# Mixture of experts on TensorE: fixed weight-stationary pairs of tiles ahead of the register-addressed blocks

## The chip, the cores and the metric

The kernel runs on one core of a Trainium2 chip. The metric is the device time of one execution, in microseconds (us). The engines are called PE (TensorE, matmuls; its weight loads are listed apart as PEld), DVE (VectorE), ACT (ScalarE), POOL (GpSimd) and SP (SyncE, which here only issues DMAs).

## What is computed

One transformer layer on 2048 tokens of width 256, all in float32: causal attention with 16 heads, a residual and a layer norm, then a mixture of experts, a residual and a second layer norm. The change touches the mixture of experts only:

```python
scores = softmax(t @ gate_w.T)            # 2048 tokens, 16 experts
weights, indices = top_k(scores, 2)
for e in range(16):                       # INTER = 176, DIM = 256
    w_e = sum(where(indices == e, weights, 0))
    y += (silu(t @ w1[e].T) * (t @ w3[e].T)) @ w2[e].T * w_e
z = (silu(t @ sw1.T) * (t @ sw3.T)) @ sw2.T    # shared expert, width 352
out = layernorm(x + y + z)
```

Every token goes to two experts, so there are 4096 rows of expert work, 256 per expert on average; how many each gets depends on the data.

## The kernel before

**Up to the experts.** Attention fills the time up to about 605 us. Its work is an order written out by hand (`steps`, `at`, lines 590 to 738); the tokens are handled in four chunks of 512, and the last chunk to be finished is chunk 2 (`LAST`). After a chunk's layer norm, `choose` and `settle` compute each token's two experts, its two gates, and its row in `xg`, a DRAM buffer with room for 2048 rows per expert. `scatter` (L275) sends the rows of 128 tokens to `xg` with one indirect DMA from POOL. A row holds 256 values, the number of the row in `yg` to which the result goes, and the token's first expert. `xg` is filled with blank rows early on (L386). The weights `w1` and `w3` of all experts come in four loads into `w13` (L370), 2 x 176 columns per expert; `w2` comes in two loads into `w2r` (L748), as two halves of 88 rows.

**Around the experts.** The shared expert's pieces (`shared_hidden`, L780, and `shared_out`, L796) serve as work for PE while something else is waited for: chunks 3 and 0 and a first piece of chunk 1 come before the experts, the rest of chunk 1 and chunk 2 after them. `shared_out` writes x + shared expert into a tile `z`. `table` (L816) works out from the counts which expert each block of 128 rows belongs to (`own`), the first row of the block in `xg` (`row`) and the number of blocks (`total`). `keys` (L852) gives each block's expert number on all partitions.

**The blocks.** An expert with n rows takes ceil(n / 128) blocks, one after the other over all experts. `in_turn` (L994) runs blocks 0 to 41 (`OFTEN` = 42), and then, under `tc.If` (L1014), blocks 42 to 46 when `total` is over 42. One block is:

- `load_block` (L867): SP loads the block's first row into a register (L868) and issues the load of 128 rows of `xg` into `xb` (L874), some eight blocks ahead (`DEPTH` = 6, eight buffers).
- `turn` (L879): two transposes on PE into `px`, one copy on DVE into `xbT`.
- `hidden` (L886): PE loads the expert's number into a register (L887); two matmuls, with `xbT` as the stationary operand and the expert's 352 columns of `w13`, addressed by that register, as the moving one, into `ph` (128 tokens x 352). ACT takes silu of the first 176 columns (`ru`, L901), DVE multiplies with the other 176 (`rh`, L903).
- `turn_hidden` (L905): two transposes of `rh` into `pT`, one ACT copy into `hT`.
- `output` (L914): two matmuls of `hT` with the expert's `w2r`, by register, into `py`; an ACT copy into `yb`; DVE works out the rows to write (`to`, L925); POOL scatters the rows into `yg` (L931). `to` and `yb` have three buffers each, so the fourth waits until a scatter has landed.

A float32 matmul of this kind is two PE instructions, a transpose is one. The program order of PE is kept (`pe`, L139, through which every matmul passes, hence line 140 in the profile); the other engines' order is chosen by the framework's scheduler. DMA loads that are marked with `keep_in_program_order` keep their order too.

**After the experts.** `fetch` (L937) loads `yg` back once all scatters have landed; `combine` (L947) adds two rows times their gates to `z` on DVE, and the layer norm and the store follow.

Of the kernel before, what the change touches and what calls it, by code (L numbers as in the profile page):

```python
# [10 lines left out]
F32 = mybir.dt.float32  # L11
I32 = mybir.dt.int32
# [15 lines left out]
NEXP, INTER, SHARED = 16, 176, 352  # L28
NF = NEXP * INTER
FTOT = NF + SHARED  # L30
HK = INTER // 2
SCH = [(0, P), (P, P), (2 * P, SHARED - 2 * P)]
NSC = len(SCH)
TT = S // P
ROW = E + 2

NBLK = (2 * S - NEXP) // P + NEXP
WARM = 3
LAST = 2
OFTEN = 42  # L40
DEPTH = 6
SCALE = 0.25
EPS = 1e-5
NEG = -1.0e30
# [3 lines left out]
def block_kernel(  # L48
# [96 lines left out]
    def transpose(*args):  # L145
        pe(nc.tensor.transpose, *args)
# [139 lines left out]
    with ExitStack() as att:  # L286
# [80 lines left out]
        for g in range(1, G):  # L367
            load_weights(g, nc.sync)
        nc.sync.dma_start(out=gw, in_=gate.rearrange("(k p) n -> p k n", p=P))
        for j, w in ((0, w1), (1, w3)):  # L370
            for k in range(2):
                nc.sync.dma_start(
                    out=w13[:, k, :, j * INTER : (j + 1) * INTER],
                    in_=w[k * P : (k + 1) * P, :NF].rearrange("p (n f) -> p n f", f=INTER),
                )

        def load_shared():
# [364 lines left out]
    fp2 = ctx.enter_context(tc.tile_pool(name="fp2", bufs=2))  # L742
    fp3 = ctx.enter_context(tc.tile_pool(name="fp3", bufs=3))
    fp4 = ctx.enter_context(tc.tile_pool(name="fp4", bufs=4))
    fp8 = ctx.enter_context(tc.tile_pool(name="fp8", bufs=8))
    ps_a = ctx.enter_context(tc.tile_pool(name="ps_a", bufs=2, space=PSUM))

    w2r = fp1.tile([HK, 2, NEXP, E], F32, tag="w2r", name="w2r")  # L748
    for j in range(2):
        nc.sync.dma_start(  # L750
            out=w2r[:, j],
            in_=w2[:NF, :].rearrange("(n j q) e -> j q n e", j=2, q=HK)[j],
        )

    blocks = fp1.tile([P, 1], F32, tag="blocks", name="blocks")
# [13 lines left out]
        out=upto, in_=upto, pattern=[[1, NEXP], [-1, NEXP]], base=0, channel_multiplier=0,  # L769
        compare_op=ALU.is_ge, fill=0.0,  # L770
    )

    z = fp1.tile([P, TT, E], F32, tag="z", name="z")

    def spare(name):
        return ps_a.tile([P, CH], F32, tag="t", name=name)

# [18 lines left out]
    def shared_out(c):  # L796
        for half in range(2):
            pz = ps_a.tile([P, 2, E], F32, tag="y", name=f"pz{c}_{half}")
            for t in range(2):
                o = (2 * half + t) * P  # L800
                for i, (_, m) in enumerate(SCH):
                    matmul(
                        pz[:, t, :], lhsT=hs[c, i][:m, o : o + P], rhs=sw2[:m, i, :],
                        start=(i == 0), stop=(i == NSC - 1),
                    )
            nc.vector.tensor_tensor(
                z[:, 4 * c + 2 * half : 4 * c + 2 * half + 2, :], pz,
                xr[c][:, 2 * half : 2 * half + 2, :E], ALU.add,
            )

    def shared(c):
        for i in range(NSC):
# [2 lines left out]

    def table():  # L816

        count = fp1.tile([P, NEXP], F32, tag="count", name="count")
        nc.vector.tensor_tensor(count, fill, room, ALU.subtract)
        whole = fp1.tile([P, NEXP], I32, tag="whole", name="whole")  # L820
        nc.vector.tensor_scalar(whole, count, float(P - 1), None, ALU.add)
        nc.vector.tensor_scalar(whole, whole, 7, None, ALU.logical_shift_right)
        nb = fp1.tile([P, NEXP], F32, tag="nb", name="nb")
        nc.vector.tensor_copy(nb, whole)
        ends = fp1.tile([P, NEXP, NEXP], F32, tag="ends", name="ends")
        nc.vector.tensor_tensor(
            ends, upto, nb.unsqueeze(1).to_broadcast([P, NEXP, NEXP]), ALU.mult
        )
        end = fp1.tile([P, NEXP], F32, tag="end", name="end")
        nc.vector.tensor_reduce(end, ends, AX.X, ALU.add)  # L830

        past = fp1.tile([P, NEXP], F32, tag="past", name="past")
        nc.vector.tensor_scalar(past, end, blocks, None, ALU.is_le)
        owner = fp1.tile([P, 1], F32, tag="owner", name="owner")
        nc.vector.tensor_reduce(owner, past, AX.X, ALU.add)
        nc.vector.tensor_tensor(past, past, nb, ALU.mult)
        first = fp1.tile([P, 1], F32, tag="first", name="first")
        nc.vector.tensor_reduce(first, past, AX.X, ALU.add)
        nc.vector.tensor_tensor(first, blocks, first, ALU.subtract)
        nc.vector.tensor_scalar(  # L840
            first, first, float(S // P - 1), float(P), ALU.min, ALU.mult
        )
        nc.vector.scalar_tensor_tensor(first, owner, float(S), first, ALU.mult, ALU.add)
        row = fp1.tile([P, 1], I32, tag="row", name="row")
        nc.vector.tensor_scalar(row, first, float(NEXP * S), None, ALU.min)
        own = fp1.tile([P, 1], I32, tag="own", name="own")
        nc.vector.tensor_scalar(own, owner, float(NEXP - 1), None, ALU.min)
        total = fp1.tile([P, 1], I32, tag="total", name="total")
        nc.vector.tensor_copy(total, end[:, NEXP - 1 :])
        return own, row, end, total  # L850
# [12 lines left out]
        return key  # L863

    xb, xbT, us, hT, expert = {}, {}, {}, {}, {}

    def load_block(b, row):  # L867
        r = nc.values_load(  # L868
            row[b : b + 1, 0:1], engines=[mybir.EngineType.SP],
            min_val=0, max_val=NEXP * S,  # L870
            skip_runtime_bounds_check_because="an expert below their number, a block of its room",
        )
        xb[b] = fp8.tile([P, ROW], F32, tag="xb", name=f"xb{b}")
        load = nc.sync.dma_start(out=xb[b], in_=xg[bass.ds(r, P), :])  # L874
        tc.keep_in_program_order(load)
        if b == 0:
            wait_for(scattered, load)

    def turn(b):  # L879
        px = ps_a.tile([P, 2, P], F32, tag="t", name=f"px{b}")  # L880
        for k in range(2):
            transpose(px[:, k, :], xb[b][:, k * P : (k + 1) * P], ident)
        xbT[b] = fp3.tile([P, 2, P], F32, tag="xbT", name=f"xbT{b}")
        nc.vector.tensor_copy(xbT[b], px)

    def hidden(b, own):  # L886
# [5 lines left out]
        for k in range(2):  # L892
# [4 lines left out]
                ],  # L897
                start=(k == 0), stop=(k == 1),
            )
        u = fp2.tile([P, INTER], F32, tag="ru", name=f"ru{b}")  # L900
        nc.scalar.activation(u, ph[:, :INTER], AF.Silu)  # L901
        us[b] = fp2.tile([P, INTER], F32, tag="rh", name=f"rh{b}")
        nc.vector.tensor_tensor(us[b], u, ph[:, INTER:], ALU.mult)  # L903

    def turn_hidden(b):  # L905
        pT = ps_a.tile([P, 2, P], F32, tag="t", name=f"pT{b}")
        for k in range(2):
            transpose(pT[:HK, k, :], us[b][:, k * HK : (k + 1) * HK], ident)
        hT[b] = fp3.tile([HK, 2, P], F32, tag="hT", name=f"hT{b}")
        nc.scalar.copy(hT[b], pT[:HK])  # L910

    back = []

    def output(b, key):  # L914
        py = ps_a.tile([P, E], F32, tag="y", name=f"py{b}")
        for k in range(2):
            matmul(
                py, lhsT=hT[b][:, k, :],
                rhs=w2r[:, k].rearrange("p n e -> p (n e)")[:, bass.ds(expert[b] * E, E)],
                start=(k == 0), stop=(k == 1),  # L920
            )
        yb = fp3.tile([P, E], F32, tag="yb", name=f"yb{b}")
        nc.scalar.copy(yb, py)  # L923
        to = fp3.tile([P, 1], I32, tag="to", name=f"to{b}")
        nc.vector.scalar_tensor_tensor(  # L925
            to, xb[b][:, E + 1 : ROW], key[:, b : b + 1], xb[b][:, E : E + 1],
            ALU.not_equal, ALU.add,
        )
        disjoint(
            back, "back",  # L930
            nc.gpsimd.indirect_dma_start(  # L931
                out=yg[:, :], out_offset=bass.IndirectOffsetOnAxis(ap=to[:, 0:1], axis=0),
                in_=yb, in_offset=None, bounds_check=2 * S - 1, oob_is_err=False,
            ).ins,
        )

    def fetch(h):  # L937

# [8 lines left out]
    def combine(h, got):  # L947
        m2 = fp2.tile([P, 2, 2], F32, tag="m2", name=f"m2_{h}")
        for t in range(2):
            i = 2 * h + t  # L950
            r = z[:, i, :]
            for j in range(2):
                nc.vector.scalar_tensor_tensor(  # L953
                    r, got[:, t, j, :], gates[:, j, i : i + 1], r, ALU.mult, ALU.add
# [10 lines left out]
        o = fp3.tile([P, 2, E], F32, tag="o", name=f"o{h}")  # L965
        for t in range(2):
            nc.scalar.activation(  # L967
                o[:, t, :], z[:, 2 * h + t, :], AF.Identity,
                bias=rs[:, 1, t : t + 1], scale=rs[:, 0, t : t + 1],
            )  # L970
        nc.sync.dma_start(
# [11 lines left out]
    settle(LAST, spare, both)  # L983
    for t in range(4):
        scatter(LAST, t)
    own, row, end, total = table()
    for b in range(DEPTH + 2):
        load_block(b, row)
    key = keys(end)
    shared_hidden(0, 1)  # L990
    shared_hidden(0, 2)
    shared_out(0)
    shared_hidden(1, 0)
    def in_turn(first, last):  # L994

        turn(first)
        turn(first + 1)
        for b in range(first, last):
            hidden(b, own)
            if b > first:  # L1000
                output(b - 1, key)
            turn_hidden(b)
            if b + 2 < last:
                turn(b + 2)
            if b + DEPTH + 2 < last:
                load_block(b + DEPTH + 2, row)
        output(last - 1, key)

    in_turn(0, OFTEN)
    blocks_in_all = nc.values_load(  # L1010
        total[0:1, 0:1], min_val=0, max_val=NBLK,
        skip_runtime_bounds_check_because="the sum of the experts' blocks, NBLK at most",
# [82 lines left out]
```

## Time and profile before

| what | value |
|---|---|
| median of 6 runs | 812.13 us (810.42 to 814.64) |
| the profiled execution: its time | 810.44 us |
| the profiled execution: its span | 808.7 us |
| mean granted clock of PE | 0.981 |
| first transpose of a block (`px`) | 640.5 us |
| first hidden matmul (`ph`) | 643.8 us |
| last output matmuls (`py`) begin | 765.3 us |
| shared expert goes on (`h`) | 767.7 us |
| scatters to `yg` | 42, the first at 650.6 us, the last at 767.1 us |
| instructions of PE | 5086 matmuls and transposes, 5086 weight loads |

The page gives busy time by engine, with the share of the span:

```profile
PE 779.4 (96%) x5086; PEld 363.2 (45%) x5086; DVE 546.5 (68%) x1489; ACT 445.2 (55%) x997; POOL 322.7 (40%) x557
```

It also cuts the span into 40 slices of 20.2 us. A digit is the busy share in tenths, and PEclk is the clock that was granted to PE. The experts are slices 32 to 38.

```profile
PE   6999999999999999999999999999999899999995
PEclk9999999999999999999999999999899999999999
DMA  5469999991000000001000000000225322222162
```

In groups and timelines a row names the line, engine and operation, the tile written and the tiles read, and the shape. A mean duration of a PE matmul is the time of its whole passage, which overlaps with the next one's.

### The profile page before, as it was taken

How to read it: one execution, taken by the hardware profiler on the slowest of the kernel's cores; microseconds unless marked ns; L12 is line 12 of the kernel's file. 1: busy time of each engine (PE TensorE's matmuls, PEld its weight loads, DVE VectorE, ACT ScalarE, POOL GpSimd, SP SyncE). 2: the span in 40 equal slices, each digit the busy share in tenths (PEclk: the TensorE clock that was granted, in tenths of full speed). 3: DMA queues.
4: the chain of work that ended last, by engine and by line, in shares of the span. 5: the costliest groups of instructions: out<-in, count | busy, mean ns of one | idle time of the engine just before them, and what ended most of it. 6: DMA issues, size and time to landing. Idle time of an engine off the chain costs nothing. (4 is left out here: it accounts for less than half of the span.)

```text
span 808.7 us, 14999 instructions
## 1 busy us (share of the span) xinstructions
PE 779.4 (96%) x5086; PEld 363.2 (45%) x5086; DVE 546.5 (68%) x1489; ACT 445.2 (55%) x997; POOL 322.7 (40%) x557
## 2 busy tenths in 40 slices
PE   6999999999999999999999999999999899999995
PEld 3443433444433344533344443453336466666543
DVE  2868888887677877688787778887575433333276
ACT  1143657387775877676786768856452033333345
POOL 2033524444454454545444545453551323333300
PEclk9999999999999999999999999999899999999999
DMA  5469999991000000001000000000225322222162
GB/s 146 130 176 328 298 292 296 305 303 46 2 1 1 2 1 2 2 19 36 1 2 1 1 2 1 1 2 27 73 62 141 111 74 86 81 85 69 36 223 90
DMA packets 67379, 71.90 MB, mean 89 GB/s; under 512 B 4736, under 2 KB 61539, under 8 KB 67302
## 3 DMA queue, kind: packets, MB, share of 16 engines
q1 hardware_dynamic: 62286, 61.77, 27.8%
q0 software_dynamic: 3552, 8.43, 3.0%
q10 hardware_dynamic: 1464, 0.72, 0.4%
q8 instruction: 42, 0.69, 0.4%
q14 instruction: 35, 0.29, 0.1%
HBM read 26.44 MB, written 45.78 MB: 89 GB/s over the span
## 5 line engine op out<-in xcount | busy, mean ns | idle before, releaser
L535 ACT ACTIVATE p<-s 128x512 f32<-128x512 f32 (+3 forms) x640 | 292.7, 540 | 132.6 <-PE m L140 77.4
L140 PE MATMUL m<-k,q 32*128 32x512 f32 (+3 forms) x1280 | 303.5, 565 | 0.8 <-DVE rot L423 0.5
L140 PE MATMUL s<-qa,k 32*128 32x512 f32 (+3 forms) x1280 | 282.4, 565 | 2.9 <-DVE avs L563 1.8
L490 DVE TENSOR_REDUCE pm<-m 128x1 f32<-128x512 f32 x384 | 237.5, 681 | 42.1 <-PE m L140 41.7
L567 POOL TENSOR_TENSOR avs<-avs,more 128x512 f32<-128x512 f32 (+3 forms) x125 | 136.8, 1094 | 166.6 <-ACT more L566 163.0
L140 PEld LDWEIGHTS s<-qa,k 32*128 32x128 f32 x1280 | 107.5, 186 | 121.0 <-ACT p L535 67.4
L140 PE MATMUL av<-p,v 128*32 128x512 f32 (+3 forms) x1280 | 156.9, 551 | 1.1 <-POOL p L539 0.7
L140 PEld LDWEIGHTS m<-k,q 32*128 32x128 f32 x1280 | 122.8, 183 | 44.0 <-issue 10.9
L485 DVE CUSTOM_DVE_ANT_0 m<-m,qmask 128x512 f32<-128x512 f32 (+3 forms) x256 | 118.2, 521 | 30.4 <-PE m L140 27.3
L566 ACT COPY more<-av 128x512 f32<-128x512 f32 (+3 forms) x125 | 65.6, 525 | 38.3 <-PE av L140 30.4
L539 POOL TENSOR_SCALAR_AFFINE_SELECT p<-p 128x128 f32<-128x128 f32 x256 | 70.3, 296 | 38.8 <-ACT p L535 36.9
L931 POOL DMA_INDIRECT yg<-yb,to x42 | 41.4, 985 | 90.0 <-ACT yb L923 49.6
L140 PEld LDWEIGHTS av<-p,v 128*32 128x32 f32 x1280 | 27.2, 109 | 105.5 <-ACT p L535 53.3
L140 PE MATMUL ph<-w,xbT 128*128 x168 | 62.0, 494 | 2.5 <-DMA xb<-xg 1.8
L903 DVE TENSOR_TENSOR rh<-ru,ph 128x176 f32<-128x176 f32 x42 | 14.2, 337 | 53.4 <-ACT ru L901 53.3
L140 PE MATMUL h<-xT,cs 128*128 128x512 f32 (+1 forms) x96 | 45.2, 616 | 3.5 <-ACT yb L923 1.3
L901 ACT ACTIVATE ru<-ph 128x176 f32<-128x176 f32 x42 | 13.3, 318 | 60.9 <-PE ph L140 60.9
L278 POOL DMA_INDIRECT xg<-xr,slot x32 | 31.0, 970 | 32.7 <-issue 21.4
L140 PE MATMUL py<-w2r,hT 88*128 x168 | 43.4, 380 | 0.7 <-ACT hT L910 0.7
L140 PEld LDWEIGHTS ph<-w,xbT 128*128 128x128 f32 x168 | 29.2, 193 | 21.3 <-issue 12.7
L428 POOL TENSOR_TENSOR k<-rot 128x512 f32<-128x512 f32 x16 | 20.3, 1266 | 43.6 <-DVE rot L426 43.6
L140 PEld LDWEIGHTS py<-w2r,hT 88*128 88x128 f32 x168 | 31.7, 189 | 12.0 <-ACT hT L910 1.2
(147 smaller groups left out, 632.1 us busy)
## 6 DMA issues: line engine op xcount, KB each, us to landing
xg<-hot SPq DMA_DIRECT2D x16, 2064.0 KB
w<-in_w_dram SPq DMA_DIRECT2D x4, 1408.0 KB
xb<-xg SPq DMA_DIRECT2D x42, 129.0 KB
got<-yg SPq DMA_DIRECT2D x8, 512.0 KB
w2r<-in_w_dram SPq DMA_DIRECT2D x2, 1408.0 KB
xr<-in_x_dram SPq DMA_DIRECT2D x4, 512.0 KB
out_dram<-o SPq DMA_DIRECT2D x8, 256.0 KB
cs<-in_rope_dram SPq DMA_DIRECT2D x16, 80.0 KB
```

What stands on the lines that cost most here:

```text
L140: tc.keep_in_program_order(op(*args, **kw))
L278: put = nc.gpsimd.indirect_dma_start(out=xg[:, :], out_offset=bass.IndirectOffsetOnAxis(ap=slot[:, j, i : i + 1], axis=0), in_=xr[c][:, t, ...
L428: nc.gpsimd.tensor_tensor(ks[g, c], tmp[:, 0, :], tmp[:, 1, :], ALU.add)
L485: nc.vector.tensor_tensor_reduce(out=ps[:, :n], in0=ps[:, :n], in1=qmask[:, CH - n :], scale=1.0, scalar=3.0 * NEG, op0=ALU.add, op1=ALU.m ...
L490: nc.vector.tensor_reduce(to, ps, AX.X, ALU.max)
L535: nc.scalar.activation(pr[:, n0:], ps[:, n0:], AF.Exp, scale=SCALE)
L539: nc.gpsimd.affine_select(out=diag, in_=diag, pattern=[[1, P]], base=0, channel_multiplier=-1, compare_op=ALU.is_ge, fill=0.0,)
L566: nc.scalar.copy(more[:, n0:], pv[:, n0:])
L567: nc.gpsimd.tensor_tensor(to, to, more[:, n0:], ALU.add)
L901: nc.scalar.activation(u, ph[:, :INTER], AF.Silu)
L903: nc.vector.tensor_tensor(us[b], u, ph[:, INTER:], ALU.mult)
L931: nc.gpsimd.indirect_dma_start(out=yg[:, :], out_offset=bass.IndirectOffsetOnAxis(ap=to[:, 0:1], axis=0), in_=yb, in_offset=None, bounds_c ...
```

## The change

The first 256 rows of every expert get a path of their own, at addresses that are known when the program is built. The pair of tiles is loaded, transposed (four transposes, one copy), and multiplied with the weights as the stationary operand and the 256 tokens as the moving one, so that the hidden values come out already turned: 112 + 64 rows of silu's argument and of the factor, in three pieces (`ab` twice, `c`). Silu and product give `hT` directly. The output matmuls take `hT` as the stationary operand, as before. The pair's results go back in two scatters. Sixteen experts run so, one after the other, with an expert's output after the next one's hidden part.

Only rows beyond 256 of an expert go through blocks with a register, by the old path. `OFTEN` is 10 now, `DEPTH` 2, and the part under `tc.If` holds blocks 10 to 27. The weight columns in `w13` are arranged as 112 + 64 + 64 + 112, so the silu of a block takes 240 columns, its product is cut in two, and the hidden transposes are of 112 and 64 columns with an ACT copy each. `w2r` is cut at 112 instead of 88, and `w13` comes in eight loads instead of four. `shared_out` adds into `xr` itself, `z` is gone. The table comes after the first four pair loads and the shared pieces in the program, and counts blocks beyond two per expert. The path is used with fewer than 256 rows too; blank rows are computed then, and not written.

```diff
-HK = INTER // 2
+H1, H2 = 112, INTER - 112
-NBLK = (2 * S - NEXP) // P + NEXP
+NBLK = 28
-OFTEN = 42
-DEPTH = 6
+OFTEN = 10
+DEPTH = 2
...
-            nc.vector.tensor_tensor(
-                z[:, 4 * c + 2 * half : 4 * c + 2 * half + 2, :], pz,
-                xr[c][:, 2 * half : 2 * half + 2, :E], ALU.add,
-            )
+            r = xr[c][:, 2 * half : 2 * half + 2, :E]
+            nc.vector.tensor_tensor(r, r, pz, ALU.add)
...
+    def load_two(e):
+        xb2[e] = fp4.tile([P, 2, ROW], F32, tag="xb2", name=f"xb2_{e}")
+        load = nc.sync.dma_start(
+            out=xb2[e], in_=xg[e * S : e * S + 2 * P, :].rearrange("(t p) r -> p t r", p=P)
+        )
+        tc.keep_in_program_order(load)
+        if e == 0:
+            wait_for(scattered, load)
+
+    def turn_two(e):
+        px = ps_a.tile([P, 2, 2, P], F32, tag="t", name=f"px2_{e}")
+        for k in range(2):
+            for t in range(2):
+                transpose(px[:, k, t, :], xb2[e][:, t, k * P : (k + 1) * P], ident)
+        xT2[e] = fp3.tile([P, 2, 2 * P], F32, tag="xT2", name=f"xT2_{e}")
+        nc.vector.tensor_copy(xT2[e], px.rearrange("p k t m -> p k (t m)"))
+
+    def hidden_two(e):
+        ab = ps_a.tile([P, 2, 2 * P], F32, tag="h", name=f"ab{e}")
+        c = ps_a.tile([P, 2 * P], F32, tag="c", name=f"c{e}")
+        for to, o, m in ((ab[:H1, 0], 0, H1), (c, H1, P), (ab[:H1, 1], INTER + H2, H1)):
+            for k in range(2):
+                matmul(
+                    to, lhsT=w13[:, k, e, o : o + m], rhs=xT2[e][:, k, :],
+                    start=(k == 0), stop=(k == 1),
+                )
+        u = fp2.tile([P, 2, 2 * P], F32, tag="u2", name=f"u2_{e}")
+        nc.scalar.activation(u[:H1, 0], ab[:H1, 0], AF.Silu)
+        nc.scalar.activation(u[:H2, 1], c[H2:], AF.Silu)
+        hT2[e] = fp2.tile([P, 2, 2 * P], F32, tag="hT2", name=f"hT2_{e}")
+        nc.vector.tensor_tensor(hT2[e][:H2, 1], u[:H2, 1], c[:H2], ALU.mult)
+        nc.vector.tensor_tensor(hT2[e][:H1, 0], u[:H1, 0], ab[:H1, 1], ALU.mult)
+
+    def output_two(e):
+        py = ps_a.tile([P, 2, E], F32, tag="y", name=f"py2_{e}")
+        for t in range(2):
+            for j, r in parts:
+                matmul(
+                    py[:, t], lhsT=hT2[e][r, j, t * P : (t + 1) * P], rhs=w2r[r, j, e],
+                    start=(j == 0), stop=(j == 1),
+                )
+        yb = fp3.tile([P, 2, E], F32, tag="yb2", name=f"yb2_{e}")
+        nc.scalar.copy(yb, py)
+        to = fp3.tile([P, 2, 1], I32, tag="to2", name=f"to2_{e}")
+        nc.vector.scalar_tensor_tensor(
+            to, xb2[e][:, :, E + 1 : ROW], float(NEXP - e), xb2[e][:, :, E : E + 1],
+            ALU.not_equal, ALU.add,
+        )
+        for t in range(2):
+            send_back(yb[:, t], to[:, t])
...
-        u = fp2.tile([P, INTER], F32, tag="ru", name=f"ru{b}")
-        nc.scalar.activation(u, ph[:, :INTER], AF.Silu)
+        u = fp2.tile([P, INTER + H2], F32, tag="ru", name=f"ru{b}")
+        nc.scalar.activation(u, ph[:, : INTER + H2], AF.Silu)
-        nc.vector.tensor_tensor(us[b], u, ph[:, INTER:], ALU.mult)
+        nc.vector.tensor_tensor(us[b][:, :H1], u[:, :H1], ph[:, INTER + H2 :], ALU.mult)
+        nc.vector.tensor_tensor(us[b][:, H1:], u[:, INTER:], ph[:, H1:INTER], ALU.mult)
...
-        for k in range(2):
-            transpose(pT[:HK, k, :], us[b][:, k * HK : (k + 1) * HK], ident)
-        hT[b] = fp3.tile([HK, 2, P], F32, tag="hT", name=f"hT{b}")
-        nc.scalar.copy(hT[b], pT[:HK])
+        hT[b] = fp2.tile([P, 2, 2 * P], F32, tag="hT2", name=f"hT{b}")[:, :, :P]
+        for (j, r), o in zip(parts, (slice(0, H1), slice(H1, INTER))):
+            transpose(pT[r, j, :], us[b][:, o], ident)
+            nc.scalar.copy(hT[b][r, j, :], pT[r, j, :])
...
+    for e in range(4):
+        load_two(e)
     shared_hidden(0, 1)
     shared_hidden(0, 2)
     shared_out(0)
     shared_hidden(1, 0)
+    own, row, end, total = table()
+    key = keys(end)
...
+    turn_two(0)
+    turn_two(1)
+    for e in range(NEXP):
+        hidden_two(e)
+        if e:
+            output_two(e - 1)
+        if e + 2 < NEXP:
+            turn_two(e + 2)
+        else:
+            turn(e + 2 - NEXP)
+        if e + 4 < NEXP:
+            load_two(e + 4)
+        elif e + 4 == NEXP:
+            for b in range(DEPTH + 2):
+                load_block(b, row)
+    in_turn(0, OFTEN, lambda: output_two(NEXP - 1))
```

## The prediction

> **What bounds the kernel now.** I read the page first: PE is busy for 96% of the span, so whatever shortens PE's own stream shortens the kernel, as long as PE also sets the end. The change lies in the expert stage, so the next view is the windows over ten blocks of it, then the timeline of one block. In the windows row the columns are the stretch, its length, and busy time with count for PE, weight loads, DVE, ACT and POOL.
>
> ```profile
> 700.00:728.60 28.60, 28.41 (x121) 18.24 (x120) 8.93 (x30) 10.20 (x30) 9.52 (x10) 1.00 0.29 83
> ```
>
> Ten blocks take 28.60 us, 2.86 us each. PE is busy throughout, the others a third of the time. But a matmul's duration is its passage through the array and overlaps the next one, so this "busy" hides small waits. The timeline shows them.
>
> ```profile
> 701.86 1.45 PE L140 MATMUL ph<-w,xbT 128*128 x4
> 703.14 1.03 PE L140 MATMUL py<-w2r,hT 88*128 x4
> 704.08 0.17 PEld L140 LDWEIGHTS pT<-ident,rh 128*88 128x88 f32 x2 [0.32 <-DVE rh L903]
> 704.08 0.42 PE L140 MATMUL pT<-ident,rh 128*88 128x128 f32 x2
> 704.34 0.38 PE L140 MATMUL px<-ident,xb 128*128 128x128 f32 x2
> 704.72 0.19 PEld L140 LDWEIGHTS ph<-w,xbT 128*128 128x128 f32 x1 [0.24 <-issue]
> ```
>
> Prices are taken start to start. The shared expert's row of eight 512-column matmuls at 636.06 lasts 3.60 us and one lasts 0.59: (3.60 − 0.59) / 7 = 0.43 us, 0.84 ns a column. So 352 columns cost 0.296, 256 columns 0.215, and a 128-column transpose (0.38 − 0.27) = 0.11. A block is 4 × 0.296 + 4 × 0.215 + 4 × 0.11 = 2.48 us of columns, and 0.38 of waiting: 0.08 for `rh` ahead of `pT`; 0.20 between the transposes and `ph`, while PE's queue loads the expert number (next row); 0.10 in the first `ph`, whose weights come late.
>
> ```profile
> L887 PEldq TENSOR_LOAD <-own x42: 298/307/491, 642.2 to 761.7; - x42
> ```
>
> The chain of waits leads through the scatters to `yg` in this stage, which looks like a POOL bound. It is not one: the last fetch needs all scatters, and each followed its block. The waits of PE from 638 to 800 name no scatter.
>
> **The change, part by part.** From the reference's inputs I work out 212 to 303 rows per expert: 41 blocks now; with the change, 16 fixed pairs and 9 blocks beyond. So 42 blocks become 16 pairs and OFTEN = 10 blocks, and the guarded part stays untaken.
>
> *Pairs.* PE per expert: 12 hidden matmuls of 256 columns, 8 output ones, 4 input transposes: 20 × 0.215 + 4 × 0.11 = 4.74 us. No hidden transpose, no register. `hT` of an expert is needed one expert later, so I expect no wait. Two old blocks cost 5.72: 16 × (4.74 − 5.72) = **−15.7**. Bounds: nothing can beat the columns; a wait of 0.3 per expert would leave −10.9.
>
> *Blocks beyond.* The built order now puts only one hidden transpose between the wait for `rh` and the next register load; the other three transposes come after the first half of `ph`. From the wait's end to `ph` was 704.72 − 704.08 = 0.64 us, of which 0.44 was transposes; now 0.11 covers it, so 0.33 is laid bare, less a little for fewer instructions issued ahead of the load. `ru` grows from 176 to 240 columns: +0.05, by ACT's 0.318 for 176 and 0.595 for 512. `rh` is cut in two and the first transpose waits for 112 columns alone: −0.07. These cancel. Two ACT copies instead of one lie under `ph`. 10 × 0.3 = **+3.0**; bounds 0 (hidden after all) and +6 (twice that).
>
> *Start.* Here DVE's order matters.
>
> ```profile
> 638.42 5.43 SPq L874 DMA_DIRECT2D xb<-xg  x7
> ...
> 640.50 0.22 DVE L925 SCALAR_TENSOR_TENSOR to<-xb,key 128x1 int32<-128x1 f32 x1 [6.15 <-DMA xb<-xg]
> ...
> 642.58 0.22 DVE L925 SCALAR_TENSOR_TENSOR to<-xb,key 128x1 int32<-128x1 f32 x1 [0.20 <-DMA xb<-xg]
> 642.71 0.68 DVE L794 TENSOR_TENSOR sh<-u,h 128x512 f32<-128x512 f32 x1
> 643.31 0.75 DVE L884 COPY xbT<-px 128x256 f32<-128x256 f32 x2
> ...
> 643.83 0.83 PE L140 MATMUL ph<-w,xbT 128*128 x2 [1.75 <-DMA xb<-xg]
> ```
>
> Three `to` wait for the first three loads at the head of DVE's queue; behind them stand `sh` and the `xbT` copy that PE waits for. In the new order **six** `to` stand there: for three pairs and for the first three blocks beyond. SP issues four double loads, then the register loads with theirs. At 0.45 us per double load (estimate from the `got` rows, four issued in 1.93 us) and 0.85 per single one (seven in 5.43), the third single issue is at about 642.6; 1.45 MB at the page's 300 GB/s lands at about 645.2, against 642.58. The `xT2` copy is 512 wide: +0.3. **+2.9**; bounds +1.5 and +5. That the table moves behind the first loads gains nothing, because the first load waited for the scatters anyway (its register was loaded at 632.1). SP's other queue entries are behind these loads.
>
> *Clock.* After that gap PE is granted half its clock:
>
> ```profile
> 641.00:644.50 3.50, 1.08 (x5) 0.69 (x6) 2.30 (x6) 0.00 (x0) 0.00 (x0) 1.00 0.57 153
> 644.60:647.90 3.30, 3.30 (x7) 1.71 (x6) 0.34 (x1) 0.32 (x1) 0.00 (x0) 0.50 0.60 157
> ```
>
> The second row (clock 0.50) costs 1.7 us now. A longer gap can lengthen the slow stretch to about 4 us of work, 2.0 lost: **+0.3**, bounds −0.7 and +1.7. [...]
>
> *Ends of the tail blocks.* First register load behind its six waits, and the last block's two `hT` copies in a row with nothing beside them: **+0.7**, an estimate from the 0.37 us copy and the 0.31 us load; bounds 0 and +1.5.
>
> *The jump.* The untaken part grows from 5 blocks to 18.
>
> ```profile
> q8 instruction: 42, 0.69, 0.4%
> ...
> 765.28 1.13 PE L140 MATMUL py<-w2r,hT 88*128 x4 [0.46 <-ACT hT L910]
> ...
> 767.67 4.84 PE L140 MATMUL h<-xT,cs 128*128 128x512 f32 x7 [1.26 <-ACT yb L923]
> ```
>
> Queue 8 brings 42 packets for PE's 10,172 matmuls and weight loads, about 242 each. The old jump passes 120 of them, half a packet; the new one 432, almost two. PE then waits 1.26 us for ACT, which covers part of a fetch. I take **+0.8**; bounds 0 and +2. [...]
>
> *At nothing.* `w13` in eight loads with shorter rows, ahead of the zero fill: that DMA stretch ends before 200 us, and the first scatter starts at 560.2. `w2r` cut at 112: loaded at 599, needed at 648.8. Sums into `xr` instead of `z`: same DVE width; the scatters they now wait for have landed, except for the last chunk's, which is added after the experts. Three more table instructions of 0.17 us run under the shared matmuls. Scatters stay 42.
>
> *Sum:* −15.7 + 3.0 + 2.9 + 0.3 + 0.7 + 0.8 = **−8.0**. The profiled run took 810.44 (span 808.7), so 802.4. The median of the runs shown is 812.13, 1.7 above it: 804.1, forecast **804**.
>
> **The rivals.**
> 1. *The give-backs stay hidden* (0.14): tail blocks at 2.86, jump covered, start +1.5. −15.7 + 1.5 + 0.7 = −13.5, 798.6. For it: queues run ahead. Against: the 0.24 "issue" wait shows that a register load is not hidden even behind four transposes.
> 2. *Half the gain goes to waits in the pairs* (0.12): 0.3 us per expert, and we are at −3.2, 809. For it: DVE's queue holds `to` of a later pair between the two halves of `hT`.
> 3. *Slower: the scatter wait* (0.11). That `to` waits until the second scatter of three pairs before has landed, and `hT` stands behind it. From the rows: `yb` ends about 0.9 us after the output, POOL takes 1.27 per scatter, landing takes 2.5 more; `hT` is then ready 5.0 us into its expert and needed at 4.74 + 2.58 = 7.3. Slack 2.3. If the pair of scatters lands more than 2.3 us later than that, PE waits; from 0.5 us per expert on, the gain is gone. With 1.0 us: −8 + 16 = +8, 820. The longest such wait is 1.2 us now (next row, total, times, longest), at one scatter per block, the same rate.
>
> ```profile
> DVE to L925 <- DMA yg<-yb,to: 16.9, 24, 1.2
> ```
>
> 4. *It does not do what it says* (0.01): more than ten blocks beyond, and the guarded 18 run: 18 × 3.15 = 57 us more. The inputs give nine.
>
> **How the numbers follow.** The forecast has 0.62, spread 800 to 808. About 0.3% (2.4 us) is what a measurement of this kernel can tell from no change. Faster: 0.62 + 0.14 + half of rival 2, 0.82; same: 0.06; slower: 0.12. The range, 798 to 811, leaves out rivals 3 and 4 and the far ends of the terms.
>
> **What would show it.** Right: in the new trace, pairs every 4.74 to 4.8 us with no `pT`; tail blocks every 3.1 to 3.2 with a wider "issue" gap ahead of `ph`; six `to` ahead of the first `xT2` copy, and `ab` starting near 646.7; a half-clock stretch after it; a gap of over 1.26 us at the jump. Wrong: pairs above 5.0, or DVE's `to` ending PE's waits; a first `ab` after 650; tail blocks near 4.

## The result and the profile after

| | before | after |
|---|---|---|
| median of the runs | 811.85 us (48 runs) | 815.13 us (22 runs) |
| ratio | | 1.0037, 95% interval 1.0028 to 1.0046 |
| profiled execution | 810.44 us, span 808.7 | 814.77 us, span 813.1 |
| up to the first hidden product of an expert | 643.83 us | 647.30 us (+3.5) |
| from there to the end of the last `py` | 122.6 us | 120.0 us (−2.6) |
| from there to the end of the span | 42.3 us | 45.8 us (+3.5) |

The change makes the kernel slower by 0.37%, where 804 us (about 1% faster) was forecast. The three parts add up to the span's +4.4 us. Start and jump were forecast as losses, though smaller ones; the expert stage, from the first hidden product to the last `py`, gained 2.6 us where 11.7 had been expected (−15.7 + 3.0 + 0.7 + 0.3).

The window over exactly five experts of the kernel after, read as in the prediction:

```profile
698.99:726.46 27.47, 27.47 (x122) 18.83 (x121) 8.07 (x21) 6.74 (x15) 9.84 (x11) 1.00 0.21 65
```

27.47 / 5 = 5.49 us per expert, at full clock and with PE "busy" throughout. The forecast had 4.74; two old blocks take 5.74. The timeline of PE over one expert:

```profile
693.50 2.48 PE L143 MATMUL py<-w2r,hT 112*128 112x256 f32 x8
695.90 0.66 PE L143 MATMUL px<-ident,xb 128*128 128x128 f32 x4
696.40 1.03 PE L143 MATMUL ab<-xT,w 128*112 128x256 f32 x4
697.26 1.03 PE L143 MATMUL c<-xT,w 128*128 128x256 f32 x4
698.13 1.03 PE L143 MATMUL ab<-xT,w 128*112 128x256 f32 x4
698.99 0.38 PE L143 MATMUL py<-w2r,hT 112*128 112x256 f32 x1
```

From the first start of a row to the next row's: the twelve hidden products take 698.99 − 696.40 = 2.59 us (12 × 0.216, as forecast), the transposes 0.50 (forecast 0.44), and the eight output products 695.90 − 693.50 = **2.40** instead of 1.72. The row's name shows the first shape only; four of the eight have 64 rows. The weight loads under it show them:

```profile
693.28 0.41 PEld L143 LDWEIGHTS py<-w2r,hT 112*128 112x128 f32 x2
694.02 0.29 PEld L143 LDWEIGHTS py<-w2r,hT 64*128 64x128 f32 x2 [0.33 <-issue]
694.65 0.30 PEld L143 LDWEIGHTS py<-w2r,hT 112*128 112x128 f32 x2 [0.33 <-issue]
695.28 0.29 PEld L143 LDWEIGHTS py<-w2r,hT 64*128 64x128 f32 x2 [0.33 <-issue]
695.90 0.42 PEld L143 LDWEIGHTS px<-ident,xb 128*128 128x128 f32 x4 [0.33 <-issue]
```

The first load follows the products with 128 rows ahead of it almost without a gap (0.04 us). At each of the four changes of rows (112 to 64, back, to 64, to 128) the load stands 0.33 us. The matmuls' start times give the price: where the rows change, the next product starts 0.31 us after the last one, and the one behind that 0.32 us later (0.165 at the transposes), where 0.215 (0.109 for a transpose) is the rule. That is 0.15 to 0.20 us per change, together 0.74 us per expert.

The start, on DVE and PE:

```profile
641.38 0.16 DVE L929 SCALAR_TENSOR_TENSOR to<-xb 128x2 int32<-128x2 f32 x1 [7.12 <-DMA xb<-xg]
...
645.74 0.22 DVE L990 SCALAR_TENSOR_TENSOR to<-xb,key 128x1 int32<-128x1 f32 x1 [0.15 <-DMA xb<-xg]
645.87 0.68 DVE L797 TENSOR_TENSOR sh<-u,h 128x512 f32<-128x512 f32 x1
646.47 1.28 DVE L899 COPY xT<-px 128x512 f32<-128x512 f32 x2
...
647.30 2.02 PE L143 MATMUL ab<-xT,w 128*112 128x256 f32 x4 [4.26 <-DVE xT L899]
```

As forecast, six `to` stand ahead of the first copy, and `ab` starts at 647.3 (forecast: near 646.7). The transposes were done at 642.1; the copy came 4.4 us later only because of the queue. Two windows of the same stretch (the eighth number is the granted clock):

```profile
641.00:646.90 5.90, 1.29 (x8) 0.84 (x8) 2.77 (x9) 0.00 (x0) 0.00 (x0) 0.81 0.90 259
647.00:651.40 4.40, 4.10 (x10) 3.19 (x11) 0.75 (x2) 0.33 (x1) 0.00 (x0) 0.50 0.14 47
```

The last output and the jump, from the timeline, and the branch's own row, from the view of that source line:

```profile
765.97 1.28 PE L143 MATMUL py<-w2r,hT 112*128 x4
...
771.85 2.04 PE L143 MATMUL h<-xT,cs 128*128 128x512 f32 x2 [4.60 <-PEq L1092]
```

```profile
L1092 PEldq COMPARE_BRANCH  x1: 4507/4507/4507, 766.9 to 766.9; - x1
```

PE's queue sat 4.5 us in one branch instruction; PE stood 4.60 us. The same row of the kernel before (line 1014) shows 0.373 us, and PE stood 1.26:

```profile
L1014 PEldq COMPARE_BRANCH  x1: 373/373/373, 765.8 to 765.8; - x1
```

Last, who PE waited for in the whole run, and the longest waits of DVE for the scatters:

```profile
PE h L143 <- PEq L1092: 4.6, 1, 4.6
PE ab L143 <- DVE xT L899: 4.3, 1, 4.3
...
PE px L143 <- DMA xb<-xg: 2.2, 2, 1.8
```

```profile
DVE to L929 <- DMA yg<-yb,to: 20.8, 13, 2.4
```

DVE waits 1.6 us at a time for scatters (20.8 us in 13 waits), as rival 3 had it, but from 650 to 733 us, where the pairs run, the trace shows no wait of PE at all, for DVE or for anything else.

### The profile page after: what moved, and what is told of

It is laid out like the page before. It is cut to its first block, busy times and chain, and to the rows that moved or that the text cites. A ratio compares the mean times of both kernels' runs of the same rounds, so it can differ in the third digit from the quotient of the medians.

```text
span 813.1 us, 14615 instructions
## 1 busy us (share of the span) xinstructions
PE 777.8 (96%) x5086; PEld 365.6 (45%) x5086; DVE 543.5 (67%) x1469; ACT 435.4 (54%) x959; POOL 322.4 (40%) x557
## 5 line engine op out<-in xcount | busy, mean ns | idle before, releaser
L497 DVE TENSOR_REDUCE pm<-m 128x1 f32<-128x512 f32 x384 | 237.8, 681 | 43.1 <-PE m L143 42.3
L143 PE MATMUL py<-w2r,hT 64*128 64x256 f32 (+3 forms) x168 | 51.9, 414 | 0.0
L143 PE MATMUL ab<-xT,w 128*112 128x256 f32 x128 | 34.2, 391 | 4.3 <-DVE xT L899 4.3
L143 PEld LDWEIGHTS py<-w2r,hT 112*128 112x128 f32 (+1 forms) x168 | 26.9, 187 | 22.1 <-issue 18.6
L492 DVE DVE_READ_ACCUMULATOR2_ANT pm<- 128x1 f32 x256 | 35.7, 139 | 0.0
L143 PE MATMUL pq<-xT,wqs 128*128 128x512 f32 x64 | 31.7, 618 | 0.0
L143 PEld LDWEIGHTS h<-xT,cs 128*128 128x128 f32 (+1 forms) x96 | 17.9, 192 | 30.2 <-issue 20.9
```

What stands on the lines that cost most here:

```text
L143: tc.keep_in_program_order(op(*args, **kw))
L492: nc.vector.tensor_tensor_reduce(out=ps[:, :n], in0=ps[:, :n], in1=qmask[:, CH - n :], scale=1.0, scalar=3.0 * NEG, op0=ALU.add, op1=ALU.m ...
L497: nc.vector.tensor_reduce(to, ps, AX.X, ALU.max)
```

## The experiments

Theory A: in the pairs, PE cannot bring the next weights forward at a change of rows down to 64 or up from it; at the jump it waits for a fetch; at the start for the six `to`. Rival B: the waits for the scatters hold the pairs. Rival C: weights as the stationary operand are slow by themselves. Three sets ran, each on a chip of its own, with runs of the kernel before beside them (medians 806.52, 813.38 and 806.04 us); ratios are against those.

**Padding the 64 rows.** Zeros in rows 64 to 127 of both operands:

```diff
+    wide = ((0, slice(0, H1)), (1, slice(0, 128)))
+    nc.gpsimd.memset(w2r[H2:128, 1], 0.0)
...
+        nc.gpsimd.memset(hT2[e][H2:128, 1], 0.0)
...
-            for j, r in parts:
+            for j, r in wide:
```

> The changed kernel with the second output product of each pair widened from 64 rows to 128: rows 64 to 127 of its two operands are filled with zeros (by POOL, off PE's stream). Same number of instructions on PE. Theory A (PE cannot bring the next weights forward where the number of rows goes down to 64 or up from it; 4 such places per expert, 0.20 + 0.20 + 0.20 + 0.15 = 0.74 us by the start times in the trace): an expert takes 4.75 us instead of 5.49, the kernel 16 x 0.74 = 11.8 us less than the changed kernel, about 803. Rival B (the waits of DVE for the scatters hold the pairs): an expert stays at 5.49, no change, 815. Rival C (weights as the stationary operand are slow by themselves, whatever their rows): no change either, 815.

Measured: 803.10 us, 0.9960 (0.9939 to 0.9981). The timeline of PE over one expert:

```profile
694.25 1.90 PE L143 MATMUL py<-w2r,hT 112*128 112x256 f32 x8
695.98 0.60 PE L143 MATMUL px<-ident,xb 128*128 128x128 f32 x4
...
699.01 1.25 PE L143 MATMUL py<-w2r,hT 112*128 112x256 f32 x5
```

An expert takes 699.01 − 694.25 = 4.76 us, its output 1.73: the forecast's own numbers, with the same count of instructions and more rows. Theory A holds, B and C fall: the scatters and the stationary weights are as they were. (That the median met the expected 803 is chance: the kernel before took 806.52 us on this chip.) The stage (first `ab` to last `py`) takes 108.4 us, 11.6 less than in the kernel after. The median fell by less: 0.9960 against 1.0037, about 6 us. Part of the gain was given back earlier, by the experiment's own filling of `w2r` on POOL, ahead of eight scatters into `xg`:

```profile
596.51 3.51 POOL L757 MEMSET w2r<- 64x4096 f32 x1 [0.52 <-PE av L143]
600.35 0.99 POOL L281 DMA_INDIRECT xg<-xr,slot  x1 [0.33 <-DVE rs L583]
```

PE then waited 3.7 us for `oh` (1.0 in the kernel after).

**Turning round the second half.**

```diff
-            for j, r in parts:
+            for j, r in parts if t == 0 else parts[::-1]:
...
-                    start=(j == 0), stop=(j == 1),
+                    start=(j == t), stop=(j != t),
```

> The changed kernel with the order of the two output products of a pair's second half turned round: rows 112, 64, 64, 112 instead of 112, 64, 112, 64. The same work. Theory A: two of the four places go (64 back to 112 between the halves, and 64 to 128 behind them becomes 112 to 128 and free), but one of the kind 64 to 112 stays: 2 x 0.20 = 0.40 instead of 0.74 us, so 5.15 us per expert and 16 x 0.34 = 5.5 us less, about 809.5. Rivals B and C: no change, 815. If the price hung on each 64-row product and not on the change of rows: no change either.

Measured: 805.20 us, 0.9983 (0.9965 to 1.0002), against 1.0037: 4.4 us less, expected 5.5, which the interval allows. The timeline gives 700.30 − 695.15 = 5.15 us per expert, as expected to the hundredth:

```profile
695.15 2.28 PE L143 MATMUL py<-w2r,hT 112*128 112x256 f32 x8
...
700.30 1.01 PE L143 MATMUL py<-w2r,hT 112*128 112x256 f32 x3
```

The same eight products cost less when the rows change twice instead of four times: 5.15 us per expert against 5.49. The price hangs on the change here, not on the 64 rows.

**64 and 65 rows in the kernel before.** `n` = 64, then 65:

```diff
-        for k in range(2):
+        for k, n in ((0, HK), (1, 64)):
             matmul(
-                py, lhsT=hT[b][:, k, :],
+                py, lhsT=hT[b][:n, k, :],
...
```

> The kernel before, with the second product of each block's output cut from 88 to 64 rows (it leaves out 24 of the 176 hidden values of each expert). Nothing else is changed. Theory A: two places per block (88 to 64 rows, and 64 to 128 ahead of the hidden transposes) at 0.20 and 0.15, of which 0.08 covers the wait for rh: 2.86 becomes 3.1 us per block, 42 x 0.27 = 11 us more than before, about 823. Rivals: fewer rows cost nothing, 812.

> As the one with 64 rows, but with 65 (leaves out 23 of 176 hidden values). If the price stands at 64 rows or fewer, as theory A has it from 112, 96 and 88 rows being free in the trace: no change, 812. If it hangs on any change of the number of rows by much, or on a count that is no multiple of 32: as with 64 rows or nearly, 820 or more.

Measured: 806.82 us, 1.0004 (0.9980 to 1.0027), with 64 rows; 806.87 us, 1.0009 (0.9987 to 1.0031), with 65. The expected 11 us did not come, and both take 2.87 us per block. Yet the weight loads of one block differ, first with 64 rows, then with 65:

```profile
702.45 0.29 PEld L140 LDWEIGHTS py<-w2r,hT 64*128 64x128 f32 x2 [0.33 <-issue]
703.07 0.17 PEld L140 LDWEIGHTS pT<-ident,rh 128*88 128x88 f32 x2 [0.33 <-DVE rh L903]
...
703.50 0.89 PEld L140 LDWEIGHTS ph<-w,xbT 128*128 128x128 f32 x4
```

```profile
700.81 0.17 PEld L140 LDWEIGHTS pT<-ident,rh 128*88 128x88 f32 x2 [0.31 <-DVE rh L903]
...
701.52 0.89 PEld L140 LDWEIGHTS ph<-w,xbT 128*128 128x128 f32 x4 [0.30 <-issue]
```

With 64 rows the price of the change is there: the load stands 0.33 us, and the products start 0.31 and 0.32 us apart. With 65 the load stands 0.03 us, and they start 0.215 to 0.22 apart. So the edge lies between 64 and 65 rows here. Upward the change to the 128 rows of `pT` mostly hides behind the wait for `rh`; in the one block without that wait it is 0.307 us from 64 rows and 0.215 from 65. But while the products are held back, PE's queue goes on to the register load. It starts 0.21 us earlier, measured from `pT`, and in both kernels the first load of `ph` follows 0.20 us after its end. So the 0.30 us "issue" wait ahead of `ph` is gone: `pT` to `ph` takes 0.43 us instead of 0.71. Of these two waits side by side only the longer is paid (2.87 us per block with either); the pairs have no other wait beside theirs. The late load came as expected, the expected price did not.

**The kernel after, and its jump.** For the second set the kernel after ran once more, beside one whose guarded part is as long as it was before:

```diff
-NBLK = 28
+NBLK = 15
```

> The changed kernel once more, so that the others of this set stand beside it on one chip. All theories: 1.0037 times the kernel before, or somewhat more on a chip where the kernel before is granted full speed after its own short gap at the start of the stage.

> The changed kernel with the guarded part cut from 18 blocks to 5, as long as it was before (it leaves out blocks 16 to 28 beyond the pairs, which these inputs never reach). Theory: the jump over about 555 PE instructions leaves the fetched code and waits for two fetches of 16 KB (PE stands 4.75 us, before 1.42), and the long stand brings one window of half clock more. With 5 blocks PE's gap is 1.4 to 1.6 us, the half-clock stretch after it 3.4 instead of 6.8 us: 3.3 + 1.4 = 4.7 us less than the changed kernel. Rival (the gap comes from ACT, which PE waits for, or from the register load ahead of the branch): the gap stays above 4 us and the time stays.

Measured: 816.47 us, 1.0035 (1.0019 to 1.0052), and 814.32 us, 1.0013 (1.0000 to 1.0027): 2 us less, about as little as these intervals can tell, expected 4.7. The gap fell as expected, from 4.45 to 1.48 us (the profiles above have 4.60 and 1.26 for the expectation's 4.75 and 1.42):

```profile
771.88 2.93 PE L143 MATMUL h<-xT,cs 128*128 128x512 f32 x3 [1.48 <-ACTq L1092]
```

The half-clock part of the expectation fell: the slow stretch behind the gap was 6.8 us here too, and 0 and 3.4 us in two later kernels with the short gap. It also matters little: in the six kernels with the short jump PE's last product ends 31.8 to 32.8 us after that `h`, and this time does not follow the slow stretch there (32.0 and 32.2 us without one, 31.8 to 32.8 with 3.4 us of it, 32.0 with 6.8). The shared products there wait for DVE as well: in the first combined kernel below, which has no slow stretch, PE waits 2.3 us for `sh`. From the end of the last `py` to the end of the span the kernels with the long jump take 44.2 to 45.8 us (seven, mean 45.0), those with the short one 42.2 to 43.1 (six, mean 42.7). That is the price at the end: 2.3 us, of 3.0 in the gap.

Does the stall grow with the distance? 36 blocks instead of 18 (one run):

> The changed kernel with a guarded part of 36 blocks instead of 18 (more than any input needs). If the stall at the jump is the fetch of the code at its target: the gap of PE stays at 4.4 to 4.8 us, with two packets of 16 KB in it. If all code passed over is fetched (one packet per some 256 instructions): two more packets, 6 to 9 us.

```profile
L1092 PEldq COMPARE_BRANCH  x1: 4117/4117/4117, 765.3 to 765.3; - x1
```

4.1 us: twice the distance, no longer stall. 811.61 us in one run settles nothing more, the packets of queue 8 (instructions) do. In all seven kernels with a long jump a 16 KB packet starts 1.1 to 1.2 us after PE reaches the branch, and the branch ends 1.3 to 1.5 us after the packet does. The packet takes 1.0 us where the branch is shortest (3.41 us, in the kernel with the second half turned round) and 2.1 us in the kernel after (4.51 us): the branch ends later where the packet does, as if PE waited for it. The packet alone is no proof: the kernel before and its two variants have one 1.2 us after the start of their branch too, and the branch has ended by then; the other three with the short jump have none there. What fills the time ahead of the packet and behind it the trace does not show.

**Holding `to` back.**

```diff
+        after(made_to, made2[e])    # made2[e]: second half of hT2[e]
...
+        after(made_to, made[b])     # made[b]: second half of us[b]
```

Here `after` adds a dependency of the first instruction on the second.

> The changed kernel with each `to` held back on DVE until the hidden values of its own pair or block are made: the six that stood ahead of the first xT2 copy come later, and none stands between the two halves of an hT any more. Theory: the copies of xT2 then follow px of the first pair at 641.4 and the shared hidden values, the first ab starts near 643.5 instead of 646.7 to 647.0: about 3.3 us less, and up to 1.7 more if one window of half clock goes with the gap. Rival (the first pair waits for its loads, not for DVE's queue): ab stays at 646 to 647, no change. Pairs stay at 5.49 us by the theory of the 64-row products; if the `to` held them up after all, they get shorter.

Measured: 808.99 us, 0.9941 (0.9925 to 0.9956): 7.6 us less than the kernel after beside it (with intervals of 0.15 to 0.17% on each ratio), more than the expected 3.3 to 5.0. The timeline:

```profile
642.09 1.42 PE L143 MATMUL px<-ident,xb 128*128 128x128 f32 x8 [1.63 <-DMA xb<-xg]
642.78 1.46 DVE L907 COPY xT<-px 128x512 f32<-128x512 f32 x2 [1.53 <-PE px L143]
643.59 0.70 PEld L143 LDWEIGHTS ab<-xT,w 128*112 128x112 f32 x4 [0.32 <-issue]
```

```profile
643.60:650.00 6.40, 6.38 (x31) 5.22 (x32) 2.64 (x7) 1.53 (x4) 0.00 (x0) 1.00 0.50 138
```

From the end of the last shared product to the first `ab` 3.2 us pass, 7.4 in the kernel after beside it and 4.2 in the kernel before. And no half-clock window follows (second fence, 1.00), worth 1.4 us there. That is 5.6 of the 7.6 us and all that the spans of the two profiled runs differ by (812.7 and 807.0); the other 2 are about what the two intervals leave open. Pairs stay at 5.49 us though no `to` stands between the halves of an `hT` any more: rival B falls a second time.

**All together.** First with the padding as above, in the blocks beyond too, the short jump, and `to` held back:

> All at once: the second output product padded with zeros to 128 rows in the pairs and in the blocks beyond, the guarded part of 5 blocks (leaving out blocks 16 to 28 beyond the pairs, which these inputs never reach), and `to` held back. Theory: the savings add up, because PE's own stream is cut in each of three places: 11.7 (pairs) + 4.7 (jump) + 3.3 (start) + 10 x 0.15 (blocks) = 21 us less than the changed kernel, 2.2 to 2.6% less, so 0.978 of the kernel before. If one hides behind another (POOL or DVE become late in the shorter pairs): 0.985 or more.

Measured: 800.69 us, 0.9844 (0.9826 to 0.9863); expected 0.978, and 0.985 or more by the rival, which comes close: POOL was late, though not in the pairs. The parts were there (4.76 per expert, gap 1.48, `ab` 3.3 us after the shared products), but POOL's filling was too, with its 3.7 us wait for `oh` and a half-clock window of 6.8 us. And the padded blocks still take 3.10 us. Without the change of rows the register load is what `ph` waits for: it starts with `pT`, and `ph` again follows 0.20 us after its end, 0.50 us from `pT`. So the last version fills `w2r` after the table and pads the pairs only:

```diff
+        after(nc.gpsimd.memset(w2r[H2:, 1], 0.0), made_row)
```

> The changed kernel with `to` held back and the second output product of the pairs padded with zeros to 128 rows, and with the zeros of w2r written by POOL only after the table, once its first scatters are issued; in the earlier padded kernels that filling took 3.5 us of POOL ahead of eight scatters, and PE then waited 3.7 instead of 1.0 us for `oh`. The guarded part keeps its 18 blocks. Theory: `to` held back measured 0.9941 of the kernel before; 16 x 0.73 = 11.7 us less on top (1.4%) and no wait for `oh` above 1.0: 0.980, about 797 where the kernel before takes 813. Rival (the pairs' saving is partly hidden elsewhere, as the 6.4 us of the first padded kernel would have it): 0.986, about 802.

> The same with a guarded part of 5 blocks (leaving out blocks 16 to 28 beyond the pairs, which these inputs never reach). Theory: PE's gap at the jump falls by 3.0 us, and the half-clock window after it was hidden behind a wait of PE for DVE: 3.0 us less than with 18 blocks, 0.976 of the kernel before. If the shorter gap is taken up by the same wait for DVE: no difference.

Measured: 792.33 us, 0.9828 (0.9802 to 0.9853), and with the short jump 791.01 us, 0.9808 (0.9783 to 0.9832). PE's waits in the two profiles, the longer jump first:

```profile
PE h L143 <- PEq L1108: 4.6, 1, 4.6
...
PE h L143 <- DVE oh L585: 1.0, 1, 1.0
```

```profile
PE h L143 <- ACTq L1108: 1.5, 1, 1.5
```

The wait for `oh` is back at 1.0, and both beat both kernels: the idea of the change is worth 1.7%, once the rows and DVE's queue are put right, with the guarded part whole. Both ratios lie 0.3 to 0.5% above the expected ones, which are just outside the intervals; the first is about midway between theory and rival. In this set the runs of the kernel before show a clock of 0.987 (median), in the second set 0.979, so there was less half clock for a shorter start gap to save; how much of the miss that explains stays open. The two versions cannot be told apart by their intervals.

## Why the prediction was wrong

| term | forecast | measured | from |
|---|---|---|---|
| pairs | −15.7 | −4.0 | 16 × (5.494 − 2 × 2.871) |
| blocks beyond, with their ends | +3.7 | +0.9 | rest of the stage |
| start | +2.9 | +3.5 | first hidden product |
| clock at the start | +0.3 | +0.4 | (4.2 − 3.4) / 2 |
| jump, to the end of the span | +0.8 | +3.5 | 45.8 − 42.3 |
| sum | −8.0 | +4.3 | the spans differ by 4.4 |

**The step that failed is "20 × 0.215 + 4 × 0.11 = 4.74 us" for a pair, "no hidden transpose, no register", with the bound "a wait of 0.3 per expert".** The count and the price per column were right, as the padded kernel shows (4.76). What was missing is the change from 112 to 64 rows and back, 0.74 us per expert, 11.8 us in all. The sum was off by 12.3 us; that the two nearly agree is luck, because the other misses (+2.7 at the jump, +0.7 at the start and its clock, −2.8 in the blocks beyond) cancel. The prices came from rows of the expert stage and of the shared expert, where the products have 88 or more rows. The trace of before had about half the price: in its attention stage a 256-column product with 32 rows is followed by one with 128 rows after 0.304 us in 16 of 17 places, where 0.215 is the rule, and a 512-column one with 128 rows by one with 64 rows after 0.522 in 18 of 20 places, where 0.429 is. The alternation, 112 and 64 rows in the inner loop of `output_two`, stood in the diff. The weight loads themselves last the same (0.18 to 0.19 us with 64 and 112 rows); what differs is when they begin: at a change of rows the load stands 0.33 us, between products with 112 or 128 rows 0.03 to 0.04. The runs show where, not why. Something else there goes with the rows: in the attention stage of before 87 of 162 products with 64 rows that follow another with 64 start 6 or 7 ns after it, and of 1001 in that trace that follow one another with 88 rows or more (and as many columns of weights) none does. What that has to do with the edge no run tests.

**Jump: wrong in size**, beyond its bound of +2: +3.5 between these two profiles, 2.3 between the kernels with the long and the short jump. That the longer jump would hold PE up was right (4.51 us in the branch, 0.37 before). The +0.8 had been scaled by the packets passed over, an estimate that no run shows: the branch took 3.4 to 4.5 us over 18 blocks and 4.1 over 36.

**Start and its clock: right**, 0.7 us small together; the order of DVE's queue was read rightly, and the experiment shows the six `to` to be the whole cause. What the prediction did not ask is whether the change needs them there. The 4 us of work at half clock were a guess that no row had given; the profile after has 4.2.

**Blocks beyond: the period was right** (3.09 us, forecast 3.15), and so was its reason: with the change of rows padded away the register load alone gives 3.10. The term was too high because the period was put on all ten blocks and +0.7 added for the ends; at the seams, periods of 2.83 and 2.88 gave it back.

**Rival 3, the slower side, is refuted as a mechanism**: the waits of DVE came (up to 2.4 us), and PE never waited for them. The kernel got slower by the change of rows, which no rival named, and by a jump beyond its bound.

## What to carry to other kernels

Before splitting a contraction unevenly, look at the number of rows of each product in order: where it goes to 64 and back, with nothing else to wait for, add 0.15 to 0.2 us per change (measured at 256 columns of float32, next to 112 and 128 rows; 0.09 from 32 to 128 rows in the attention stage), or pad with zeros, group, or turn the order round. Price a product from a row of the same shape and the same neighbours, wherever in the trace it stands, and look at where a scheduler puts cheap instructions that wait for transfers in an engine's queue (six of them kept the first copy on DVE 4.4 us behind its transposes here). A jump held PE's queue up for 3.4 to 4.5 us here, whether it passed 18 blocks or 36, and not when it passed 5 (0.37 us in the kernel before, 0.25 in the one after with the short jump); 2.3 us of it reached the end.

## What the runs showed of the hardware beyond that

- The row count shows an edge between 64 and 65, in either direction (upward from 65 to 128 in one place only): 0.31 us from start to start where 64 follows 88 rows, and where 128 follows 64. 65 after 88 and ahead of 128, and 96 and 112 on either side of 128, cost nothing: 0.215 us from start to start with 256 columns.
- Half the clock does not follow every gap. From the end of the shared products to the first product of an expert, a gap of 3.4 us brought one window of 3.4 us in the last version with the guarded part whole, and gaps of 3.2 to 3.4 us none in three others; 4.2 us brought one in the kernel before, and 4.0 and 4.2 none in its two variants; 7.2 to 7.7 us brought two in all six kernels that have it. At the short jump 1.3 to 1.5 us brought none, one or two.
- The median of the unchanged kernel differs between sets by 0.9% (806.04 to 813.38 us), more than the effect of the change; only ratios within a set carry over.
